# The second batch's order of attention steps: pair 8-9 first by seven half-size products, pair 6-7 scored in one step

## The chip, the cores and the metric

The kernel runs on one core of a Trainium2 chip. The metric is the device time of one execution in microseconds; the median of several runs of the kernel before is 1007.96 us. Traces count time from the start of the profiled span, and all positions below are given on that scale.

## The reference, cut to what matters

One layer on `x` of shape (2, 2048, 512), in float32: a layer norm, then a causal single-head attention and a mixture-of-experts network side by side, then a gated sum.

```python
xn = layernorm(x)
# attention (with a layer norm of its own ahead of q, k, v)
q, k, v = norm(xn) @ Wq, norm(xn) @ Wk, norm(xn) @ Wv
scores = where(causal, q @ k.T / sqrt(512), -inf)
s = softmax(scores) @ v @ o_proj + xn
# mixture of experts: top 2 of 8, y = w2 @ silu(w1 @ xn + b1) + b2
g = silu(moe(xn))
out = x + s * g
```

The change touches the attention of the second batch only: scores, softmax and the product with the values.

## The kernel before, in words

The first 567 us compute norms, projections and the experts. Then comes the attention, a loop over steps `s = 0..31`, one for each tile of 128 query rows; `seq[s]` says which tile it is. Steps 0 to 15 are the first batch, from its last tile to its first; steps 16 to 31 are the second batch, in the order 8, 9, 0, 1, 6, 7, 2, 3, 4, 5, 10 to 15. Tiles come in pairs, and two steps of one pair share the query tile `q`. Keys and values lie in blocks of 512 rows (`aks`, `avs`); tile t needs the first t + 1 groups of 128 keys.

There is no planner: each engine has a queue that it works through in the order in which the Python loop writes its instructions, and it stops at an instruction whose inputs are not there. What follows is the order of an ordinary step s. TensorE writes the scores of tile s into PSUM, chunk by chunk (`chunk_scores`, L1307), and VectorE masks the last chunk (L1312) and takes a maximum of each (`maximum`, L1295). VectorE writes the probabilities of step s - 1, which have come back transposed from a DMA, into the tile `pT` (`join_p`, L1517). Then come the row maximum `nm` (`end_scores`, L1395) and the divisor of the step before (L1659, L1660), and `exponentials`: ScalarE's exponential (L1485), GpSimd's split of the result into 16-bit halves (`pu`, L1495), and SyncE's DMA transposes (`puT`, L1501). TensorE multiplies with the values two steps late (`values`, L1535). Tiles with at most three groups of keys are turned on TensorE instead (`turn_p`, L1512). Beside this run, for older tiles: `attended` (ScalarE L1696, then VectorE L1699), `emit` (GpSimd L1707, L1708, then a store), and once for a pair `gather_y` (GpSimd's indirect DMAs, L1678) and `gate` (ScalarE L1688, VectorE L1689, ScalarE's Silu L1691).

Some pairs are multiplied by Strassen's scheme in Winograd's form, with seven half-size products for eight.

- Scores: pairs in `SCORED` take the first two key blocks by `fast_scores` (products L1359, sums of their results on VectorE L1365, one copy on ScalarE L1378). It needs sums of the key blocks (`block_sums`, tile `tk`, L1340: four subtractions, once for a batch) and of the queries (`query_sums`, tile `sq`, L1326 to L1329, once for a pair). `pair 13`, steps 26 and 27, is the first of the second batch.
- Values: pairs in `FAST` (those, and pair 4) wait until both tiles are there. `combine_p` forms sums of the two `pT` tiles (L1577, four instructions), `combine_v` those of the value blocks (tile `vT`, L1557). `values_first`, `values_next` (both in the step after the pair) and `values_end` (one step later) run seven chains of products (L1583), with VectorE's sums of the results (L1600) and one ScalarE copy (L1611).

PSUM is shared by two pools: `ps_a`, five banks, for scores and transposes, and `ps_b`, three banks, for values. Work that a later pair needs is placed by step number in the table `later`: `block_sums` of the second batch stands at steps 20 to 23, the last `combine_v` at 24 to 27.

Of the kernel before, what the change touches and what calls it, by code (L numbers as in the profile page):

```python
# [26 lines left out]
def gated_attention_moe(  # L27
# [32 lines left out]
    NT = B * S // P  # L60
    BT = 4
    TB = BT * P
    NB = NT // BT
    NBB = S // TB
# [947 lines left out]

    assert B == 2 and NBB == 4
    seq = [t for t in reversed(range(NBB * BT))]
    seq += [NBB * BT + t for t in (8, 9, 0, 1, 6, 7, 2, 3, 4, 5, 10, 11, 12, 13, 14, 15)]
    assert all(seq[s] // 2 == seq[s + 1] // 2 for s in range(0, NT, 2))
    fetch_k = fetch(aks, lambda: kp2, kt_d, "k2", "kT")
    fetch_v = fetch(avs, lambda: vp, v_d, "v2", "v")
# [249 lines left out]
    OUT = 4  # L1268


    SCORED = (0, 1, 2, 3, 13, 14, 15)
    FAST = SCORED + (4,)

    def place(s):
        b, t = divmod(seq[s], BT)
        return b, t, b - b % NBB
# [21 lines left out]
    def direct(s):  # L1298

        return range(2 if s // 2 in SCORED else 0, len(widths[s]))  # L1300

    def chunk_scores(s, j):
        b, t, first = place(s)
        w = widths[s][j]
        ps = ps_a.tile([P, TB], F32, name=f"ps_{s}_{j}", tag="a")
        for c in range(ND):
            nc.tensor.matmul(  # L1307
                ps[:, :w], lhsT=aqs[seq[s] // 2][:, c, ts(t % 2, P)], rhs=aks[first + j][:, c, :w],
                start=(c == 0), stop=(c == ND - 1),
            )  # L1310
        if first + j == b:
            nc.vector.tensor_tensor(ps[:, w - P : w], ps[:, w - P : w], keep, ALU.min)  # L1312
        maximum(s, ps[:, :w], j * TB)
# [79 lines left out]
    def end_scores(s):  # L1393
        mx, nm, pieces = scored[s]
        nc.vector.tensor_reduce(nm, mx[:, : len(pieces)], AX.X, ALU.max, negate=True)  # L1395
# [23 lines left out]
    for i in range(NM):  # L1419
# [21 lines left out]
        for _ in range(3):  # L1441
            if i >= paired.stop and early:
                f, b, c = early.pop(0)
# [115 lines left out]
    def combine_p(s, parts=(1, 3, 2, 4)):  # L1559

        m = min(min(place_keys(s), place_keys(s + 1)) // 2, MOST)
        a1, a2 = (
            turned[s + i][:, : 2 * m * P].rearrange("p (k h q) -> p k h q", h=2, q=P)
            for i in range(2)
        )
        a11, a12, a21, a22 = a1[:, :, 0], a1[:, :, 1], a2[:, :, 0], a2[:, :, 1]
        if 1 in parts:
            psums[s] = [
                cp.tile([P, MOST, P], F32, name=f"s{i}_{s}", tag=f"s{i}")[:, :m] for i in (1, 2, 4)
            ]  # L1570
        s1, s2, s4 = psums[s]
        for i, dst, x1, x2, op_ in (
            (1, s1, a21, a22, ALU.add), (3, a21, a11, a21, ALU.subtract),
            (2, s2, s1, a11, ALU.subtract), (4, s4, a12, s2, ALU.subtract),
        ):
            if i in parts:
                nc.vector.tensor_tensor(dst, x1, x2, op_)  # L1577
        combos[s] = m, a11, a12, a22, s1, s2, a21, s4
# [160 lines left out]
    K = NBB  # L1739
# [6 lines left out]
    later = {}  # L1746
    for steps, f, b in (
        ((10, 10, 11, 11), combine_v, K + 2), ((12, 12, 13, 13), combine_v, K + 1),
        ((20, 21, 22, 23), block_sums, K), ((24, 25, 26, 27), combine_v, K),
    ):  # L1750
        for i, step in enumerate(steps):
            later.setdefault(step, []).append((f, b, (i + 1,)))
# [6 lines left out]

    for s in range(NT + OUT + 2):  # L1760
        fast = s // 2 - 1 in FAST
        pair = (s, s + 1) if s // 2 in SCORED else (s,)
        if s < NT and (s % 2 == 0 or len(pair) == 1):
            for k in pair:
                if s:
                    begin_scores(k)
                room(k)
        n = s // 2 + 1
        if s % 2 == 0 and NQ <= n < NT // 2:
            for c in range(2):  # L1770
                fetch_q(n, c)
        if s == 0:
            fetch_parts(s, NBB * ND)
            block_sums(0)
        late = []
        for k in range(NT):
            if k not in AHEAD:
                wait = 4 - k % 2 if k // 2 in FAST else 3
                if s == k + wait:
                    late.append((attended, k))  # L1780
                if s == k + wait + 1:
                    emit(k)
        if s == NT:

            values_first(s - 2)
            for k in AHEAD:
                make_ahead(k)
        if len(pair) == 1 or s % 2:
            for f, *args in late:
                f(*args)  # L1790
        for k in range(NT):
            if s == (NT - 1 if k in AHEAD else k + 2 - k % 2 if k // 2 in FAST else k + 1):
                fetch_inputs(k)
        if s == NT - 1:
            gather_y(NT - 2)
        if s % 2 and s > 3 and s // 2 + 1 in SCORED:
            query_sums(s + 1, nc.vector)
        joins = []
        for k in () if s == 1 else (0, 1) if s == 2 else (s - 1,):
            if 0 <= k < NT - 1 and not by_te(k):  # L1800
                joins += [(join_p, k)] * len(halves[k])
        chunks = []
        if s < NT and s != 1:
            chunks = [(k, j) for k in ((1,) if s == 0 else (s,)) for j in direct(k)]
        if s == 0:

            for k, j in chunks:
                chunk_scores(k, j)
            chunks = []
        if s < NT and s % 2 == 0 and len(pair) == 2:  # L1810
            pools = [(ps_a, "a")] * 5 + [(ps_b, "b"), (ps_a, "a")]
            if s < 3:
                pools = [(ps_b, "b")] * 3 + [(ps_a, "a")]
            if s == 2:
                joins = [(combine_v, b, (1,)) for b in range(NBB - 1)] + joins
            now = 5 if s == 2 else 1
            fast_scores(s, pools, late + joins[:now])
            joins = joins[now:]
            if s == 0:
                query_sums(2, nc.gpsimd)  # L1820
        for k, j in chunks:
            chunk_scores(k, j)
            if s != 3 and joins:
                f, *args = joins.pop(0)
                f(*args)
        if s != 3:
            for f, *args in joins:
                f(*args)
        if 0 <= s - 1 < NT and by_te(s - 1):

            if not fast:
                values(s - 2)
            turn_p(s - 1)
        if s < NT and s != 1:
            end_scores(s)
        if fast and s % 2 == 0 and 2 < s < NT:
            combine_p(s - 2)
        if 0 <= s - 1 < NT:
            divisor(s - 1)
        if s < NT:  # L1840
            if s != 1:
                exponentials(s)
            if s % 2 == 0 and len(pair) == 2:
                maximum(s + 1, turned[s + 1][:, : 2 * TB], 0)
            if s == 0:
                end_scores(1)
                exponentials(1)
            fetch_parts(s, 4)
            for f, *args in later.pop(s, []):
                f(*args)  # L1850
        if s == 2:
            pass
        elif s == 3:
            combine_p(0, (1, 3, 2))
            for b in range(NBB - 1):
                combine_v(b, (2,))
            values_first(0)
            combine_p(0, (4,))
            for b in range(NBB - 1):
                combine_v(b, (4,))  # L1860
            values_next(0)
            for f, *args in joins:
                f(*args)
            values_end(0, [lambda: query_sums(s + 1, nc.vector)])
        elif s == NT:
            emit_ahead(s - 2, seven[s - 2][1], LO)
            values_next(s - 2)
        elif fast and s % 2 == 0:
            values_first(s - 2)

            if s != NT - 2:
                values_next(s - 2)
        elif fast and s == NT - 1:
            values_next(s - 3)
            values_end(
                s - 3,
                [lambda: join_p(s)] * len(halves[s])
                + [lambda: combine_p(s - 1, (1, 3)), lambda: gate(s - 1)]
                + [lambda: combine_p(s - 1, (2, 4))],
            )  # L1880
        elif fast:
            values_end(s - 3)
        elif 0 <= s - 2 < NT and not (s - 1 < NT and by_te(s - 1)):
            values(s - 2)

        for k in range(0, NT - 2, 2):
            if s == (k + 2 if k + 2 in AHEAD else k + 3):
                gate(k)
        for k in range(0, NT - 2, 2):
            if s == k + 1:  # L1890
                gather_y(k)
        if s == 1:

            for b in (2, 0, 1):
                combine_v(b, (3,), nc.gpsimd)
# [45 lines left out]
```

## Time and profile before

| | |
|---|---|
| runs, us | 1007.8, 1007.96, 1009.46 |
| profiled execution, us | 1007.83 |
| its span, us | 1006.0 |
| granted TensorE clock | 1.000 |
| busy: PE, VectorE, ScalarE, GpSimd | 99%, 71%, 40%, 48% |
| attention begins at | 568 us |
| second batch's first score product | 777.11 us |

In the groups and the timeline, PE is TensorE's matmul, PEld its weight load, DVE VectorE, ACT ScalarE, POOL GpSimd, and SPq the DMA queue of SyncE. A line of the timeline holds the start, the length, the engine, the source line, the operation, what it writes and reads, and how many were merged; in brackets stands the idle time before it and what ended it. A matmul's length includes the time it takes to drain, so lines of PE overlap by about 0.16 us when one follows the other at once; a break shows as a gap in the starts. One product in the source is two instructions on PE.

### The profile page before, as it was taken

The page shows a single profiled execution, that of the slowest core. Times are in us where ns is not written, and L with a number is a line of the kernel's source. Part 1 is how long each engine was busy: PE and PEld are TensorE (multiplying, and loading weights), DVE is VectorE, ACT ScalarE, POOL GpSimd, SP SyncE. Part 2 cuts the span into 40 slices and gives each one's busy share as a digit, 9 for nine tenths or more (in the row PEclk, how much of TensorE's full clock was granted, in tenths as well). Part 3 has the DMA queues.
Part 4 walks back from the last instruction along what each step waited for, and adds up shares of the span by engine and source line. Part 5 has one row for each costly group of instructions (what it writes and reads, how often), then busy time and mean ns, then how long its engine had stood idle before and what let it go on. Part 6 is the DMA issues. An engine that isn't in the chain of part 4 may idle for free. (4 is left out here: it accounts for less than half of the span.)

```text
span 1006.0 us, 13431 instructions
## 1 busy us (share of the span) xinstructions
PE 999.9 (99%) x3924; PEld 665.3 (66%) x3924; DVE 716.9 (71%) x1396; ACT 403.2 (40%) x804; POOL 483.3 (48%) x475
## 2 busy tenths in 40 slices
PE   9999999999999999999999999999999999999998
PEld 5888888874567767766753448677675544447577
DVE  6996746897887777677744579668576556878667
ACT  3344445322444454444445112232335535442241
POOL 4474564004644454444332165254557776764272
PEclk9999999999999999999999999999999999999999
DMA  8689996978999999999999576274677768753361
GB/s 293 193 264 293 329 286 258 349 249 240 202 227 220 211 208 221 217 200 222 216 218 242 164 193 147 78 206 104 183 199 239 225 200 240 207 141 86 92 165 42
DMA packets 296647, 207.96 MB, mean 207 GB/s; under 512 B 230776, under 2 KB 243832, under 8 KB 296576
## 3 DMA queue, kind: packets, MB, share of 16 engines
q1 hardware_dynamic: 282432, 163.56, 63.2%
q0 software_dynamic: 10400, 34.63, 12.5%
q10 hardware_dynamic: 3744, 8.91, 2.4%
q8 instruction: 34, 0.56, 0.2%
q14 instruction: 37, 0.30, 0.1%
HBM read 92.35 MB, written 60.03 MB: 151 GB/s over the span
## 5 line engine op out<-in xcount | busy, mean ns | idle before, releaser
L1195 PE MATMUL py<-arena,ht 128*128 (+3 forms) x396 | 176.7, 593 | 0.0
L1307 PE MATMUL ps<-k,q 128*128 128x512 f32 (+3 forms) x416 | 143.0, 495 | 0.3 <-PEq L1455 0.3
L1495 POOL COPY pu<-pT 128x1024 uint16<-128x1024 uint16 (+2 forms) x74 | 82.5, 1146 | 118.1 <-ACT pT L1485 59.1
L1166 POOL COPY hu<-h 128x704 uint16<-128x704 uint16 x66 | 61.9, 956 | 155.8 <-issue 121.7
L1195 PEld LDWEIGHTS py<-arena,ht 128*128 128x128 f32 (+3 forms) x396 | 71.8, 185 | 80.7 <-issue 76.9
L1307 PEld LDWEIGHTS ps<-k,q 128*128 128x128 f32 x416 | 74.7, 190 | 67.1 <-issue 56.5
L970 POOL DMA_INDIRECT xs<-zu_d,toki x66 | 77.6, 1176 | 70.2 <-DVE toki L791 55.6
L1181 ACT ACTIVATE ht<-ht,b1sel 128x128 f32<-128x128 f32 (+3 forms) x216 | 67.9, 380 | 88.1 <-DVE ht L1175 88.1
L1145 DVE TENSOR_TENSOR h<-p,h 128x176 f32<-128x176 f32 x182 | 55.5, 337 | 60.7 <-PE p L1138 57.2
L1678 POOL DMA_INDIRECT yg<-y_d,posi x64 | 67.4, 1053 | 36.9 <-DVE yg L1689 21.9
L1535 PE MATMUL po<-v,pT 128*128 128x512 f32 x152 | 67.9, 592 | 0.0
L347 POOL COPY zu<-z 128x1024 uint16<-128x1024 uint16 x32 | 39.9, 1245 | 55.7 <-DVE z L332 55.7
L1517 DVE COPY pT<-puT 128x1024 uint16<-128x1024 uint16 (+2 forms) x74 | 54.1, 759 | 8.8 <-DMA puT<-pu 8.6
L1485 ACT ACTIVATE pT<-pT,nm 128x1024 f32<-128x1024 f32 x14 | 16.1, 1148 | 110.3 <-DVE nm L1395 72.0
L1203 ACT COPY y<-py 128x512 f32<-128x512 f32 x55 | 32.2, 585 | 62.3 <-PE py L1195 48.4
L1485 ACT ACTIVATE pT<-ps,nm 128x512 f32<-128x512 f32 (+3 forms) x52 | 30.1, 581 | 62.5 <-DVE nm L1395 38.8
L1365 DVE TENSOR_TENSOR pT<-p,pT 128x512 f32<-128x512 f32 x49 | 32.9, 687 | 25.8 <-PE p L1359 22.1
L1535 PEld LDWEIGHTS po<-v,pT 128*128 128x128 f32 x152 | 28.6, 190 | 31.9 <-issue 30.1
L1707 POOL TENSOR_TENSOR o<-o,yg 128x512 f32<-128x512 f32 x30 | 42.0, 1398 | 14.3 <-DVE o L1699 14.1
L1699 DVE SCALAR_TENSOR_TENSOR o<-xo,xscale,o 128x512 f32<-128x512 f32 x30 | 25.9, 871 | 30.1 <-ACT o L1696 30.1
L1046 DVE COPY xT<-xhT 128x1024 uint16<-128x1024 uint16 x66 | 45.2, 712 | 2.3 <-DMA xhT<-xs 2.0
L1708 POOL TENSOR_TENSOR o<-o,xo 128x512 f32<-128x512 f32 x30 | 43.0, 1432 | 2.4
(342 smaller groups left out, 2142.9 us busy)
## 6 DMA issues: line engine op xcount, KB each, us to landing
y_d<-y SPq DMA_DIRECT2D x66, 256.0 KB, 4.4
zu_d<-zu SPq DMA_DIRECT2D x32, 264.0 KB, 2.8
kt_d<-kT SPq DMA_DIRECT2D x16, 512.0 KB, 5.9
q<-qt_d SPq DMA_DIRECT2D x32, 256.0 KB, 5.4
k<-kt_d SPq DMA_DIRECT2D x32, 256.0 KB, 4.7
v<-v_d SPq DMA_DIRECT2D x32, 256.0 KB, 5.6
xo<-in_x_dram SPq DMA_DIRECT2D x32, 256.0 KB, 3.8
x<-in_x_dram SPq DMA_DIRECT2D x30, 256.0 KB, 4.9
```

Of the source, the lines that this page charges most:

```text
L970: nc.gpsimd.indirect_dma_start(out=xs, out_offset=None, in_=zu_d, in_offset=bass.IndirectOffsetOnAxis(ap=toki[:, order[i] : order[i] + 1], ...
L1046: nc.vector.tensor_copy(xT.bitcast(U16).rearrange("p c (t h) -> p c t h", h=2), xhs.pop(i).rearrange("p (h c) t -> p c t h", h=2),)
L1145: nc.vector.tensor_tensor(out, x, y, ALU.add)
L1166: nc.gpsimd.tensor_copy(hu[:, :, :H], h.bitcast(U16).rearrange("p (d h) -> p h d", h=2))
L1181: nc.scalar.activation(ht[:hn, c, at], ht[:hn, c, at], AF.Silu, bias=b1sel[:hn, c, j : j + 1])
L1195: nc.tensor.matmul(py[at, :], lhsT=ht[:k, c, at], rhs=rhs[n], start=(c == 0), stop=(c == NH - 1),)
L1307: nc.tensor.matmul(ps[:, :w], lhsT=aqs[seq[s] // 2][:, c, ts(t % 2, P)], rhs=aks[first + j][:, c, :w], start=(c == 0), stop=(c == ND - 1),)
L1485: nc.scalar.activation(turned[s][:, at:end], src, AF.Exp, bias=nm, accum_out=rs[:, j : j + 1])
L1495: nc.gpsimd.tensor_copy(pu[:, : 2 * w].rearrange("p (h d) -> p h d", h=2), turned[s][:, k : k + w].bitcast(U16).rearrange("p (d h) -> p h ...
L1517: nc.vector.tensor_copy(turned[s][:, k : k + w].bitcast(U16).rearrange("p (i t h) -> p i t h", t=P, h=2), puT[:, : 2 * w // P, :].rearrang ...
L1535: nc.tensor.matmul(dst, lhsT=turned[s][:, ts(k, P)], rhs=avs[first + k // BT][:, k % BT, cols], start=(start and k == k0), stop=(k == k1 - 1),
L1678: nc.gpsimd.indirect_dma_start(out=y, out_offset=None, in_=y_d, in_offset=bass.IndirectOffsetOnAxis(ap=posi[k][:, n : n + 1], axis=0),)
```

## The change

The second batch is taken in the order 8, 9, 6, 7, 0, 1, 4, 5, 2, 3, 10 to 15. Pair 8 (steps 16 and 17, tiles 8 and 9) enters `SCORED`, and with it `FAST`: its scores and its values are formed by seven half-size products. `block_sums` and the last `combine_v` move ahead, to steps 14 to 17, and `query_sums` of the pair comes in step 15. Pair 9 (steps 18 and 19, tiles 6 and 7) is `JOINT`: both of its score tiles are computed in step 18, and what step 18 did for older tiles (`attended`, the joins of step 17 and the `combine_p` of pair 8) is written between the exponentials of the first and the scores of the second.

```diff
-    seq += [NBB * BT + t for t in (8, 9, 0, 1, 6, 7, 2, 3, 4, 5, 10, 11, 12, 13, 14, 15)]
+    seq += [NBB * BT + t for t in (8, 9, 6, 7, 0, 1, 4, 5, 2, 3, 10, 11, 12, 13, 14, 15)]
...
-    SCORED = (0, 1, 2, 3, 13, 14, 15)
+    SCORED = (0, 1, 2, 3, 8, 13, 14, 15)
     FAST = SCORED + (4,)
+    JOINT = (9,)
...
-        ((20, 21, 22, 23), block_sums, K), ((24, 25, 26, 27), combine_v, K),
+        ((14, 14, 15, 15), block_sums, K), ((16, 16, 17, 17), combine_v, K),
...
-        pair = (s, s + 1) if s // 2 in SCORED else (s,)
+        joint = s < NT and s // 2 in JOINT
+        pair = (s, s + 1) if s // 2 in SCORED or joint else (s,)
...
-            chunks = [(k, j) for k in ((1,) if s == 0 else (s,)) for j in direct(k)]
+            here = () if joint else (1,) if s == 0 else (s,)
+            chunks = [(k, j) for k in here for j in direct(k)]
...
-        if s < NT and s % 2 == 0 and len(pair) == 2:
+        if joint and s % 2 == 0:
+            for k in pair:
+                for j in direct(k):
+                    chunk_scores(k, j)
+                end_scores(k)
+                exponentials(k)
+                if k == s:
+                    for f, *args in late + joins:
+                        f(*args)
+                    joins = []
+                    if fast:
+                        combine_p(s - 2)
+        if s < NT and s % 2 == 0 and s // 2 in SCORED:
...
-        if s < NT and s != 1:
+        if s < NT and s != 1 and not joint:
             end_scores(s)
-        if fast and s % 2 == 0 and 2 < s < NT:
+        if fast and s % 2 == 0 and 2 < s < NT and not joint:
             combine_p(s - 2)
...
-            if s != 1:
+            if s != 1 and not joint:
                 exponentials(s)
-            if s % 2 == 0 and len(pair) == 2:
+            if s % 2 == 0 and s // 2 in SCORED:
                 maximum(s + 1, turned[s + 1][:, : 2 * TB], 0)
```

## The prediction

> **What bounds the kernel now.** I read the page first, then TensorE alone in the timeline, then all engines around 777 us, where the second batch's scores begin.
>
> ```profile
> PE 999.9 (99%) x3924; PEld 665.3 (66%) x3924; DVE 716.9 (71%) x1396; ACT 403.2 (40%) x804; POOL 483.3 (48%) x475
> PEclk9999999999999999999999999999999999999999
> PE 43%; DVE 1%; issue 0%
> ```
>
> TensorE is busy throughout at full clock, and the chain that ended last is TensorE's. So TensorE work that goes is time won, unless TensorE comes to wait. The timeline says how close that is.
>
> ```profile
> 749.20 1.03 PE L1535 MATMUL p<-v,pT 128*128 128x256 f32 x4
> 750.65 1.56 PE L1583 MATMUL p<-vT,pT 128*128 128x256 f32 x6 [0.43 <-DVE u L1600]
> ...
> 773.42 1.06 PE L1307 MATMUL ps<-k,q 128*128 128x128 f32 x8
> ...
> 777.11 7.92 PE L1307 MATMUL ps<-k,q 128*128 128x512 f32 x24
> 784.87 1.88 PE L1535 MATMUL po<-v,pT 128*128 128x512 f32 x4
> ```
>
> The 0.43 us at 750.65 is TensorE's only wait in the attention. From 777.11 on it has none: each line starts 0.16 us before the former ends. The other engines have spare time on average, but VectorE's is in pieces, and GpSimd takes part of it:
>
> ```profile
> 774.54 1.27 POOL L1707 TENSOR_TENSOR o<-o,yg 128x512 f32<-128x512 f32 x1
> 775.89 1.26 POOL L1708 TENSOR_TENSOR o<-o,xo 128x512 f32<-128x512 f32 x1
> 776.74 0.96 DVE L1699 SCALAR_TENSOR_TENSOR o<-xo,xscale,o 128x512 f32<-128x512 f32 x1 [1.92 <-ACT o L1696]
> ...
> 862.80 1.44 POOL L1707 TENSOR_TENSOR o<-o,yg 128x512 f32<-128x512 f32 x1
> 863.04 1.48 DVE L1328 TENSOR_TENSOR sq<-q 128x256 f32<-128x256 f32 x1
> 864.32 1.33 POOL L1708 TENSOR_TENSOR o<-o,xo 128x512 f32<-128x512 f32 x1
> 864.45 1.48 DVE L1329 TENSOR_TENSOR sq<-q,sq 128x256 f32<-128x256 f32 x1
> ```
>
> A `sq` subtraction takes 0.41 us alone (at 889.99), here 1.48: each ends 0.28 after the GpSimd instruction beside it (864.24 to 864.52; 865.65 to 865.93). GpSimd's add in turn ends 1.13 after `sq` (864.52 to 865.65). They alternate.
>
> **The change part by part.** A product of 512 columns is two instructions 0.429 us apart (eight take 3.43), so 0.858 us.
>
> *Removed from TensorE.* Scores of pair 8 over two blocks: 16 products become 14. Values: 16 of 512 columns over eight key groups become 28 of 256. Each saves 2 x 0.858; together **-3.43 us**. Everything else on TensorE is the same work in another order. The changed kernel's list of instructions has the seven products where the text says, so the change does what it says.
>
> *Added and moved, first wait: key and query sums (steps 14, 15).* VectorE gets two `tk` in step 14, four `sq` and two `tk` in step 15; before, the `tk` stood in steps 20 to 23, with nobody waiting. Now the third product (780.54 without a wait) needs the second `sq`, the fourth the third `tk`. A `tk` is 1.21 us:
>
> ```profile
> L1340 DVE TENSOR_TENSOR tk<-k,tk 128x1024 f32<-128x1024 f32 x2 | 2.4, 1206 | 0.0
> ```
>
> VectorE is free at 774.82 (end of step 14's L1660). Walk: `tk` waits for GpSimd until 775.81, ends 776.89; GpSimd's add until 778.02; second `tk` 779.10; L1699 779.80; `sq` 780.15; GpSimd's multiply (it needed that L1699) 781.28; second `sq` 781.56. Third product at 781.6, 1.1 us late. GpSimd's add 782.69; third and fourth `sq` 782.97, 783.3; step 15's small row work (1.0) 784.3; the last two `tk` run beside indirect DMAs, where the trace has a value subtraction at its bare 0.68 (769.15): 785.4 and 786.55. Fourth product at 785.5, another 2.1 us late. The seventh ends at 792.35 instead of 789.1: **+3.25**. Without any collision VectorE would have the third `tk` at 781.6, before the fourth product (782.26): 0.
>
> Here a rule speaks against the change. The Trainium skill, "SBUF — State Buffer", section "Who interferes with whom", says that a VectorE instruction with two SBUF inputs and a GpSimd one that reads SBUF exclude each other for a whole instruction. The rows agree on who waits, but not on the price: a blocked `sq` ends 0.28 after the release, not 0.41, a blocked add 1.13, not 1.26. By the rule alone the seven turns above would cost 0.9 us more; I take the rows.
>
> *Second wait: values of pair 8.* Before, step 18 took tiles 16 and 17 by plain `values`. Now `values_next` needs both rows transposed and summed. The chain: after the fourth `tk` come two L1689 (1.4), Silu (1.06) and the ScalarE copy of the first product (0.57, queued behind it), ending 789.5; five sums 3.41; L1699 0.75; sum, maximum over 1024, sum 2.35; mask, maximum, `nm` 0.8: exponentials of row 16 at **E = 796.85**. What follows from there is in the trace of the same tile:
>
> ```profile
> 788.48 0.69 ACT L1485 ACTIVATE pT<-ps,nm 128x512 f32<-128x512 f32 x1
> 789.32 2.82 POOL L1495 COPY pu<-pT 128x1024 uint16<-128x1024 uint16 x3 [1.35 <-ACT pT L1485]
> 790.38 3.90 SPq L1501 DMA_TRANSPOSE puT<-pu  x3
> 793.69 1.57 DVE L1517 COPY pT<-puT 128x1024 uint16<-128x1024 uint16 x1 [1.21 <-DMA puT<-pu]
> ```
>
> The third transpose starts some 4.55 after the exponential and lands 3.3 later (790.38 to 793.69). In VectorE's queue the row maximum of row 17 stands behind the three joins of row 16, so row 17's exponential starts at E + 8.9 to 9.4. In the new order ScalarE then has two L1688, a table load, Silu, another table load, two exponentials of tile 6, and only then L1696 of step 15; VectorE's L1699 waits for it, with the joins of row 17 queued behind:
>
> ```profile
> 869.22 1.33 ACT L1688 ACTIVATE yg<-yg,share 128x512 f32<-128x512 f32 x2
> 870.57 1.28 ACT L1691 ACT_TABLE_LOAD   x1
> 871.86 1.06 ACT L1691 ACTIVATE yg<-yg 128x1024 f32<-128x1024 f32 x1
> ```
>
> 1.6 (rest of row 17) + 1.35 + 1.3 + 1.0 + 1.3 + 1.25 + 0.75 + L1699 0.75 + joins 1.65 + first L1577 0.69 = 11.6. So the first sum stands at E + 20.5 to 21; each GpSimd instruction met in the joins and sums adds up to 1.1, and three may be met (E + 24.4). I take one: E + 22.1 = 819.0. TensorE without waits would want it at 777.11 + scores 12.0 + rest of steps 16 and 17 5.3 + both tiles of pair 9 12.9 + `values_first` 3.9 = 811.1. So TensorE is 7.9 late there, **4.65 more** than after the first wait. A smaller first wait doesn't help: E comes from VectorE.
>
> *Third wait.* The fourth value bank reuses the first, which is read last by L1600 behind three more L1577 (2.0), tile 7's maxima (1.8), its exponentials and the L1611 copy (1.8) and itself 0.4, all after the first sum: 6.0 against TensorE's 5.15: **+0.8**.
>
> *Moves at no cost.* Later `tk` and `vT` leave steps 20 to 27, where TensorE waited for nothing: no gain. The tiles in steps 20 to 25 keep 10 to 12 us of TensorE work between scores and values; tile 6 before had 12.3 with its join 1.2 us early, so 0 to 1 us may be lost at tile 4. The pair's `xo` loads and four `pu` and transposes change places in GpSimd's and SyncE's queues; no queue gets more. K and `q_8` are read by TensorE at 777.11 before as well. The `q` of pair 9 is issued in step 16, some 12 us ahead of use; loads of `q` there took 5.7 to 8.5.
>
> **Sum.** -3.43 + 3.25 + 4.65 + 0.8 = +5.3 us. The profiled execution took 1007.83 (span 1006.0 and 1.8 around it), 0.1 under the median: **1013.1 us**. Bounds of the unknown: no collision at all gives E = 793.3 and the first sum at 814.1, so 3.0 + 0.8 - 3.43 = +0.4; all collisions give a first sum at 821.3, so 10.2 + 1.5 (the third wait with one collision of its own) - 3.43 = +8.3.
>
> A second rule weighs on this. The skill's "TensorE: Matmul & The Clock Gate", section "Part 1: The HAM clock gate", says that an idle window of about 3.4 us halves the clock for about 3.4 us. PEclk is 9 in all slices, but the trace has no wait above 0.43 here. By the trace the second wait costs its 4.65, by the rule up to 1.7 to 3.4 more. I leave it out of the sum and put it in the range.
>
> **The rivals.**
>
> - *The cover holds (faster).* One mechanism: the 13.7 us of TensorE work between row 17's last scores and `values_first` (po, then pair 9) covers the chain of row 17. It decides at about 813.7: with the first sum there before, waits stay under 3.43 less the 0.8; at 811 the whole gain stays, 1004.5 us. For it: VectorE idles over a quarter of the time, and before, pair 26-27 ran without a wait. Against: there TensorE had 21.5 us from the end of 27's scores (887.9) to its `values_first` (909.40), and even my walk without collisions ends at 814.1. Chance 0.13.
> - *About even.* Few collisions, +0.4: 1006 to 1010 us. Chance 0.15.
> - *Waits as worked out*, 1010 to 1015.5 us, likeliest 1013.1. Chance 0.55.
> - *Long waits and the clock.* All collisions, plus up to 3.4 for the clock: 1016 to 1020 us. Chance 0.17.
>
> **How the numbers follow.** A measurement can tell 0.2%, about 2 us, from no change. Faster by more 0.13, within 0.15, slower 0.72. The range 1006.5 to 1017.5 leaves a tenth out on either side.
>
> **What would show it.** Right: TensorE gaps of about 1 and 2 us ahead of the third and fourth product (`tk`, `sq` named), one of 4 to 5 us ahead of the first L1583 with `s` in steps 18 and 19, behind L1577, and under 1 us ahead of the fourth bank; L1699 of step 15 just ahead of row 17's joins. Wrong: no gap at L1583, or gaps in steps 20 to 25, which I take as covered.

## The result, and the profile after

The changed kernel takes 1022.89 us (median of 4 runs, 1022.58 to 1023.2), the kernel before 1008.38 us beside it (4 runs, 1007.8 to 1009.46). The ratio is 1.0143, 95% interval 1.0125 to 1.016: 14.5 us slower, where 5 us slower (1013.1, range 1006.5 to 1017.5) was forecast. The sign was right, the size was not.

The profiled execution took 1023.07 us with a span of 1021.4. Line numbers of the changed kernel are one higher than those of the kernel before (L1699 is now L1700). From the page: engines, granted clock in 40 slices, and the chain that ended last.

```profile
PE 1002.0 (98%) x3950; PEld 672.5 (66%) x3950; DVE 736.7 (72%) x1417; ACT 403.3 (39%) x802; POOL 481.5 (47%) x475
PEclk9999999999999999999999999999999979999999
PE 30%; issue 5%; DVE 4%; POOL 4%; ACT 1%; DMA 1%; POOLq 0%; DVEq 0%; ACTq 0%
```

The 7 in the clock row is new, and the chain, TensorE's almost alone before, now also runs over VectorE and GpSimd. A row's busy time hides this: TensorE is still 98% busy. Its timeline (start, length, line, tiles, count; in brackets the wait ahead and what ended it) shows where:

```profile
783.69 1.99 PE L1360 MATMUL p<-tk,sq 128*128 128x512 f32 x4 [1.98 <-DVE sq L1328]
786.56 3.67 PE L1360 MATMUL p<-tk,sq 128*128 128x512 f32 x8 [0.88 <-DVE tk L1341]
...
823.77 3.75 PE L1584 MATMUL p<-vT,s 128*128 128x256 f32 x8 [8.03 <-DVE s L1578]
827.32 3.15 PE L1584 MATMUL p<-vT,pT 128*128 128x256 f32 x8
830.30 1.89 PE L1584 MATMUL p<-vT,s 128*128 128x256 f32 x8
...
868.33 4.53 PE L1536 MATMUL po<-v,pT 128*128 128x512 f32 x10
...
878.77 5.39 PE L1536 MATMUL po<-v,pT 128*128 128x512 f32 x12 [2.48 <-DVE pT L1518]
```

Beyond the bracket, each wait also cost the 0.16 us by which lines otherwise overlap. So the waits, counted from start to start, are 2.1 and 1.1 at the scores of pair 8, 8.2 at its values, 0.2 at tile 4 (868.33, too short for a bracket) and 2.6 at tile 5: 14.3 us. Then the eight instructions at 823.77 and the eight at 827.32: from start to start they take 3.55 and 2.98 us, against 1.72 at full speed. The stretches around it give the clock (columns: stretch, length, busy time and count of TensorE, its weight loads, VectorE, ScalarE, GpSimd, then the granted clock, DMA share and GB/s):

```profile
798.60:823.70 25.10, 17.13 (x51) 9.31 (x49) 19.66 (x28) 10.80 (x19) 19.44 (x16) 0.92 0.60 156
823.70:830.30 6.60, 6.53 (x17) 5.27 (x18) 4.89 (x11) 2.81 (x7) 1.97 (x2) 0.53 0.52 65
830.30:850.00 19.70, 19.70 (x74) 13.25 (x73) 12.59 (x24) 6.29 (x9) 14.07 (x12) 1.00 0.69 217
```

After the long wait TensorE ran at about half clock, which cost 1.83 + 1.26 = 3.1 us. Taken microsecond by microsecond, the granted clock fell inside the wait, some 4 us after its start (0.80 in 819 to 820), stayed at 0.50 and was back in 829 to 830 (0.58): 10.2 us in all, 6.1 of them with products to do, and half of 6.1 is the 3.1 lost. Sum: 14.3 + 3.1 - 3.43 = 14.0 of the 15.4 us by which the spans differ. Another 1.0 us of the 15.4 lies ahead of every changed step (the value product with a small wait stands at 751.65, at 750.65 before), and 0.4 I can't place.

What the long wait waits for is on VectorE and GpSimd (lines of all engines, in order of time):

```profile
808.89 3.03 POOL L1496 COPY pu<-pT 128x1024 uint16<-128x1024 uint16 x3 [2.16 <-ACT pT L1486]
809.93 2.54 DVE L1690 SCALAR_TENSOR_TENSOR yg<-yg,share,yg 128x512 f32<-128x512 f32 x2 [0.93 <-ACT yg L1689]
...
816.16 0.94 POOL L1679 DMA_INDIRECT yg<-y_d,posi  x1 [0.30 <-issue]
816.91 2.04 DVE L1700 SCALAR_TENSOR_TENSOR o<-xo,xscale,o 128x512 f32<-128x512 f32 x1 [2.86 <-ACT o L1697]
817.12 1.27 POOL L1708 TENSOR_TENSOR o<-o,yg 128x512 f32<-128x512 f32 x1
818.47 1.60 POOL L1709 TENSOR_TENSOR o<-o,xo 128x512 f32<-128x512 f32 x1
818.88 4.15 DVE L1518 COPY pT<-puT 128x1024 uint16<-128x1024 uint16 x3
820.02 2.72 POOL L1496 COPY pu<-pT 128x1024 uint16<-128x1024 uint16 x2
822.95 0.68 DVE L1578 TENSOR_TENSOR s<-pT 128x512 f32<-128x512 f32 x1
```

Read it from below. The first sum of rows, L1578, stands behind three joins, these behind L1700, and L1700 behind ScalarE, as forecast. But the VectorE instructions on the way up to the sum lie beside GpSimd ones and take longer than alone: the two L1690 beside three copies of exponentials (L1496), L1700 beside the multiply L1708, the joins beside the add L1709 and two more copies. L1690 and L1700 each end about 0.6 us after the GpSimd instruction beside them.

### The profile page after: what moved, and what is told of

Its sections match the earlier page's. It is cut to its first block, busy times and chain, and to the rows that moved or that the text cites. A ratio compares the mean times of both kernels' runs of the same rounds, so it can differ in the third digit from the quotient of the medians.

```text
span 1021.4 us, 13507 instructions
## 1 busy us (share of the span) xinstructions
PE 1002.0 (98%) x3950; PEld 672.5 (66%) x3950; DVE 736.7 (72%) x1417; ACT 403.3 (39%) x802; POOL 481.5 (47%) x475
## 5 line engine op out<-in xcount | busy, mean ns | idle before, releaser
L1496 POOL COPY pu<-pT 128x1024 uint16<-128x1024 uint16 (+3 forms) x74 | 81.5, 1134 | 123.3 <-ACT pT L1486 63.6
L1308 PE MATMUL ps<-k,q 128*128 128x512 f32 (+3 forms) x384 | 129.1, 487 | 0.3 <-PEq L1456 0.3
L1308 PEld LDWEIGHTS ps<-k,q 128*128 128x128 f32 x384 | 68.7, 190 | 59.8 <-issue 48.3
L1518 DVE COPY pT<-puT 128x1024 uint16<-128x1024 uint16 (+3 forms) x74 | 59.5, 836 | 10.1 <-DMA puT<-pu 9.0
L1366 DVE TENSOR_TENSOR pT<-p,pT 128x512 f32<-128x512 f32 x56 | 37.5, 686 | 28.1 <-PE p L1360 18.6
L1536 PE MATMUL po<-v,pT 128*128 128x512 f32 x114 | 51.4, 594 | 2.5 <-DVE pT L1518 2.5
L1486 ACT ACTIVATE pT<-ps,nm 128x512 f32<-128x512 f32 (+3 forms) x48 | 27.3, 571 | 61.5 <-DVE ri L1660 34.2
L1584 PE MATMUL p<-vT,s 128*128 128x256 f32 x180 | 43.7, 391 | 8.0 <-DVE s L1578 8.0
L1708 POOL TENSOR_TENSOR o<-o,yg 128x512 f32<-128x512 f32 x30 | 42.4, 1413 | 15.3 <-DVE o L1700 15.1
L1700 DVE SCALAR_TENSOR_TENSOR o<-xo,xscale,o 128x512 f32<-128x512 f32 x30 | 29.4, 990 | 23.6 <-ACT o L1697 21.7
L1360 PE MATMUL p<-tk,sq 128*128 128x512 f32 x96 | 42.8, 594 | 2.9 <-DVE sq L1328 2.0
```

The source lines that it names most:

```text
L1308: nc.tensor.matmul(ps[:, :w], lhsT=aqs[seq[s] // 2][:, c, ts(t % 2, P)], rhs=aks[first + j][:, c, :w], start=(c == 0), stop=(c == ND - 1),)
L1360: nc.tensor.matmul(ps, lhsT=x[:, c], rhs=y[:, c], start=(c == 0), stop=(c == ND // 2 - 1))
L1496: nc.gpsimd.tensor_copy(pu[:, : 2 * w].rearrange("p (h d) -> p h d", h=2), turned[s][:, k : k + w].bitcast(U16).rearrange("p (d h) -> p h ...
L1518: nc.vector.tensor_copy(turned[s][:, k : k + w].bitcast(U16).rearrange("p (i t h) -> p i t h", t=P, h=2), puT[:, : 2 * w // P, :].rearrang ...
L1536: nc.tensor.matmul(dst, lhsT=turned[s][:, ts(k, P)], rhs=avs[first + k // BT][:, k % BT, cols], start=(start and k == k0), stop=(k == k1 - 1),
L1584: nc.tensor.matmul(dst, lhsT=a[:, k], rhs=v(k), start=(k == 0), stop=(stop and k == n - 1))
```

## Experiments

Each is an edit of the changed kernel; ratios are to the kernel before, run beside it.

### The order alone, and the values alone

Which part of the loss belongs to the seven products, which to the order? First the new order and the joint step with pair 8 scored and valued plainly:

```diff
-    SCORED = (0, 1, 2, 3, 8, 13, 14, 15)
+    SCORED = (0, 1, 2, 3, 13, 14, 15)
-        ((14, 14, 15, 15), block_sums, K), ((16, 16, 17, 17), combine_v, K),
+        ((20, 21, 22, 23), block_sums, K), ((24, 25, 26, 27), combine_v, K),
```

> The new order and the joint step for tiles 6 and 7 alone: pair 8-9 by plain products, key sums back at steps 20 to 23, value sums at 24 to 27. Theory Q (the waits come from VectorE's queue: key and query sums in steps 14 and 15, joins and sums of pair 8 in step 18): no TensorE wait in steps 14 to 19, full clock; only tile 5's late joins (2.65 us in the changed kernel at 878.77) may remain. 1008 to 1011 us. Rival R (the new order or the joint step itself costs): over 1015 us, with waits in steps 18 and 19.

Measured: 1010.98 us, ratio 1.0035 (1.0014 to 1.0056). TensorE doesn't wait in steps 14 to 19, and the clock stays at 1.00. The order has a price of its own, about 3 us, at tiles 4 and 5:

```profile
857.24 3.24 PE L1536 MATMUL po<-v,pT 128*128 128x512 f32 x7 [1.04 <-DVE pT L1518]
...
865.96 5.39 PE L1536 MATMUL po<-v,pT 128*128 128x512 f32 x12 [0.75 <-DVE pT L1518]
```

The first line stops at the edge of its view; tile 4 has ten such instructions. Two more waits of 0.4 follow at 906 and 917. Next, scores of pair 8 by seven but values plain:

```diff
-    FAST = SCORED + (4,)
+    FAST = tuple(p for p in SCORED if p != 8) + (4,)
```

> As changed, but the values of pair 8 by plain products (scores still by seven). Theory Q: the first wait (3.3 us) stays. The wait of 8.2 us for the sums of the two probability tiles goes, since tile 8's values need row 16 alone; tile 9's values then start about 819.4 and row 17's joins ended at 823.0 in the changed kernel, so 0 to 3.6 us are waited there. Plain values cost 1.7 us. With the clock's 3.1 us gone: 1022.9 - 8.2 - 3.1 + 1.7 + 0 to 3.6 = 1013.3 to 1016.9 us. Rival (the time is lost in the scores, not in the values): 1020 us or more.

Measured: 1014.58 us, ratio 1.0068 (1.0045 to 1.0091). The long wait is gone; the first wait and tile 5's 2.6 stay. Here the first wait was followed by slow products:

```profile
783.33 2.59 PE L1360 MATMUL p<-tk,sq 128*128 128x512 f32 x4 [1.99 <-DVE sq L1328]
786.20 4.56 PE L1360 MATMUL p<-tk,sq 128*128 128x512 f32 x8 [0.28 <-DVE tk L1341]
```

In the changed kernel the same four and eight took 1.99 and 3.67 after an equal wait. The granted clock in 783 to 791 was 0.79 here (first row), 1.00 there (second row; columns as above):

```profile
783.00:791.00 8.00, 7.39 (x13) 2.84 (x14) 6.27 (x14) 5.17 (x8) 2.95 (x4) 0.79 0.85 285
783.00:791.00 8.00, 6.43 (x15) 2.76 (x16) 6.27 (x14) 5.06 (x8) 3.15 (x3) 1.00 0.80 273
```

So the clock fell around a wait of 2 us in one execution and not in the other. With plain values the loss is 6.8 us (before: 1007.75 beside it), in all 14.5, so about half of it comes with the seven products' values. The runs of this version lie 5 us apart, so the share is not known better than that.

### The clock by itself

If 3.1 us is the clock and not the wait, dummy products that fill the wait must give it back though nothing arrives sooner.

```diff
         p57 = bank(s, "p57")
+        if s == NT // 2:
+            for k in range(16):
+                nc.tensor.matmul(
+                    p57[:, LO], lhsT=combos[s][1][:, k % 4], rhs=raw(s, 0, LO)(k % 4),
+                    start=True, stop=True,
+                )
```

> As changed, but TensorE works in the long wait: 16 products of 256 columns (6.9 us) whose results the next chain overwrites stand ahead of pair 8's third chain. Theory C (the wait of 8.2 us lowers the clock, and the eight products after it pay 3.1 us): the clock stays at 1.00, the wait shrinks to about 1.3 us, nothing else moves: 1022.9 - 3.1 = 1019.8 us. Rival (the slow products after the wait have another cause, their inputs or a port): 1022.9 us, the same slow products.

Measured: 1021.68 us, but between 1018.26 and 1023.52; ratio 1.0127 (1.0108 to 1.0145). In the profiled run (1023.52, the slowest of the four) the products after the wait are at full speed:

```profile
824.02 1.99 PE L1584 MATMUL p<-vT,s 128*128 128x256 f32 x8 [0.21 <-DVE s L1578]
...
830.05 1.13 PE L1536 MATMUL p<-v,pT 128*128 128x256 f32 x4 [0.58 <-DVE o L1601]
```

From `p57` to the scores of step 20 the run needs 12.1 us, the changed kernel 13.9: 3.1 won on the clock, part of it given back by a wait for L1601, and a small one after it, that the slow products had covered. But in this run the clock fell elsewhere, to 0.79 in 783 to 791 and 0.83 in 876 to 886, at the other two waits. So all waits were filled next: 4 and 2 dummies ahead of the third and fourth product of pair 8, the 16 as above, 4 at tile 5.

```diff
+            for _ in range({3: 4, 4: 2}.get(count[0], 0) if s == NT // 2 else 0):
+                nc.tensor.matmul(ps[:, LO], lhsT=a11[:, 0], rhs=b11[:, 0, LO], start=True, stop=True)
...
+        for _ in range(4 if s == 23 else 0):
+            nc.tensor.matmul(
+                po[:, LO], lhsT=aqs[seq[25] // 2][:, 0, :P], rhs=aks[NBB][:, 0, LO],
+                start=True, stop=True,
+            )
```

> The changed kernel with dummy products in the waits: 4 and 2 of 256 columns ahead of the third and fourth score product of pair 8, 16 ahead of the seven products' values, 4 ahead of tile 5's values; their results are overwritten. If what remains of the scatter and of the loss is the clock that falls after each wait: the granted clock is 1.00 in every slice, the waits as seen on TensorE are filled, and every run lies at 1018 to 1019.5, with less than 1 us between them. Rival (the clock is not what scatters): 1021 to 1023, or runs 3 us or more apart, as with the dummy products in the long wait alone.

Measured: 1019.52 us (1018.91 to 1020.56), ratio 1.0097 (1.0067 to 1.0127), mean clock 1.00. The runs lie 1.65 us apart; less than 1 was expected. The clock's share of the loss is 1022.89 - 1019.52 = 3.4 us (3.7 if each is taken against its own runs of before), against 3.1 in the trace.

### VectorE's queue and GpSimd's turns

Two causes were left for the long wait. By theory P it is made of VectorE's collisions with GpSimd (the two engines hold each other up when they work at the same time); by theory S of latency and queue order. First, the multiply by the gate and the sum with x left out in steps 12 to 15 (the output of those tiles lacks both):

```diff
+        if not 12 <= s < 16:
             nc.gpsimd.tensor_tensor(o, o, g, ALU.mult)
             nc.gpsimd.tensor_tensor(o, o, xt, ALU.add)
```

> As changed, but GpSimd's multiply and add (the gate and the sum with x) are left out for the tiles of steps 12 to 15, so their output lacks them. Theory P (GpSimd and VectorE exclude each other, and that is most of both waits): the first wait goes (third key sum at about 782.6, needed at 783.3), row 16's exponentials start near 794.3 and not 798.6, the long wait falls from 8.2 to about 3 and keeps the clock: 1022.9 - 3.3 - 5.2 - 3.1 = 1011.3 us. Rival S (the order of VectorE's and ScalarE's queues alone makes the waits): 1019 us or more, with a long wait of 6 us or more.

Measured: 1016.65 us, ratio 1.0087 (1.007 to 1.0104), between the two theories. The long wait falls by 3.0, to 5.1 (the profiled run, 1019.24, is the slowest of four):

```profile
819.87 3.65 PE L1584 MATMUL p<-vT,s 128*128 128x256 f32 x8 [4.98 <-DVE s L1578]
```

The first wait stayed at 2.1: its collisions are with tiles of steps 10 and 11, outside the range that I had chosen. Then the queue: joins and sums of rows ahead of the attended values' scaling.

```diff
-                    for f, *args in late + joins:
+                    for f, *args in joins:
                         f(*args)
                     joins = []
                     if fast:
                         combine_p(s - 2)
+                    for f, *args in late:
+                        f(*args)
```

> As changed, but in step 18 the joins of row 17 and the sums of pair 8 stand ahead of attended of step 15, not behind it. Theory Q1 (the joins had landed and stood in VectorE's queue behind the multiply-add of attended, which waited for ScalarE's gate, two table loads and two exponentials): joins begin near 814 and not 818.9, first sum near 817 to 818, the wait of 8.2 us falls to 2 to 3.5, its clock penalty mostly goes: 1013 to 1017 us. Rival (the transposes land late, or GpSimd holds VectorE wherever the joins stand): a wait of 6 us or more, 1020 us or more.

Measured: 1020.31 us (1016.96 to 1021.01), ratio 1.0115 (1.0098 to 1.0132); less gain than expected. The trace is of the fastest run, 1016.96. The joins now start at 812.43 instead of 818.88 (all of this run lies 1.4 us earlier), but the wait only falls to 4.5:

```profile
812.43 1.31 DVE L1518 COPY pT<-puT 128x1024 uint16<-128x1024 uint16 x2
...
815.19 2.19 DVE L1518 COPY pT<-puT 128x512 uint16<-128x512 uint16 x1 [1.46 <-DMA puT<-pu]
815.82 1.27 POOL L1708 TENSOR_TENSOR o<-o,yg 128x512 f32<-128x512 f32 x1
817.17 1.33 POOL L1709 TENSOR_TENSOR o<-o,xo 128x512 f32<-128x512 f32 x1
817.31 1.75 DVE L1578 TENSOR_TENSOR s<-pT 128x512 f32<-128x512 f32 x1
```

A join of 512 columns takes 0.43 alone (at 811.14 in the last run of this series), a sum 0.68: the collisions had moved to them. And VectorE now stands idle for 1.46 us until the third transpose has landed, a part of the wait that is latency, as theory S has it. So both at once, and over all steps concerned. First the multiply and add left out in steps 10 to 23 instead of 12 to 15 (the output of those tiles lacks both, here and in the two runs that follow):

```diff
+        if not 10 <= s < 24:
             nc.gpsimd.tensor_tensor(o, o, g, ALU.mult)
             nc.gpsimd.tensor_tensor(o, o, xt, ALU.add)
```

> The changed kernel with GpSimd's multiply by the gate and sum with x (L1708, L1709 of the changed kernel) left out for the tiles of steps 10 to 23; the output of those tiles lacks the gate and the sum with x. Theory P (the collisions with GpSimd on VectorE are most of what the forecast missed): the two waits at the scores of pair 8 shrink to 0 to 0.5 us, the exponentials of row 16 start about 4 us earlier on the kernel's scale, the wait ahead of L1584 falls from 8.0 to 3 to 4 us (the place of the joins behind L1700 remains), tile 5's wait from 2.5 to 1 or less, and the clock keeps 0.9 or more in those slices: 1010 to 1013 us. Rival S (it is latency and the order of VectorE's queue, collisions are beside the point): the wait ahead of L1584 stays at 5 us or more and the time is 1017 or more.

Measured: 1013.99 us, ratio 1.0047 (1.0037 to 1.0056). The first wait is gone, tile 5's is 0.8 instead of 2.6, but the long one is 5.1, not 3 to 4. GpSimd had nothing else to do, so its copies moved up beside L1700:

```profile
812.54 2.54 DVE L1700 SCALAR_TENSOR_TENSOR o<-xo,xscale,o 128x512 f32<-128x512 f32 x1 [2.86 <-issue]
...
812.72 1.81 POOL L1496 COPY pu<-pT 128x1024 uint16<-128x1024 uint16 x2
```

Then the same with the joins ahead:

> As the run without GpSimd's two instructions in steps 10 to 23 (same part of the output left out), and with the joins of pair 8 and its sums of rows put ahead of the attended values' scaling in step 18. If queue place and collisions are the two causes and there is no third: the wait ahead of L1584 is 1.5 us or less and the time is 1006 to 1010. If a third remains (landing of the transposes, or the latency of the exponentials): the wait is 3 us or more, and the time not over 1 us below the run without the move.

Measured: 1011.16 us, ratio 1.0026 (1.0016 to 1.0035). Neither forecast was met: 2.8 us were won, but a wait of 3.2 remained. Most of it has the same cause in a new place:

```profile
811.48 2.78 DVE L1578 TENSOR_TENSOR s<-pT 128x512 f32<-128x512 f32 x1
...
811.90 1.80 POOL L1496 COPY pu<-pT 128x1024 uint16<-128x1024 uint16 x2
...
814.40 3.45 PE L1584 MATMUL p<-vT,s 128*128 128x256 f32 x8 [3.08 <-DVE s L1578]
```

So the two copies of step 18 went to ScalarE:

```diff
-                nc.gpsimd.tensor_copy(
+                (nc.scalar.copy if s == 18 else nc.gpsimd.tensor_copy)(
```

> The run with both changes (L1708 and L1709 left out in steps 10 to 23, so that those tiles lack the gate and the sum with x; joins and sums of rows ahead of the attended values' scaling), and with the two copies of the exponentials of step 18 (L1496) moved from GpSimd to ScalarE. In the run with both changes the first sum of rows (L1578) took 2.78 us in place of 0.68, beside these two copies, 811.90 to 813.70. If VectorE's collisions with GpSimd's copies are the third cause: the first sum takes 0.7 us, the wait ahead of L1584 is 1.0 us or less, the clock stays at 1.00 there, and the time is 1007 to 1009 (2.1 less for the sum, up to 1.6 less for the clock). Rival (the last transpose's landing and latency hold the sums): the wait stays at 2.5 us or more and the time at 1010.5 to 1012.

Measured: 1008.05 us, ratio 0.9997 (0.9988 to 1.0006): no difference left to the kernel before. The sum takes its bare 0.68, the wait is 1.2 (VectorE idles 1.35 for the third transpose), the clock 1.00 throughout:

```profile
811.48 0.68 DVE L1578 TENSOR_TENSOR s<-pT 128x512 f32<-128x512 f32 x1
...
812.31 1.97 PE L1584 MATMUL p<-vT,s 128*128 128x256 f32 x8 [1.03 <-DVE s L1578]
...
818.86 1.13 PE L1536 MATMUL p<-v,pT 128*128 128x256 f32 x4 [1.13 <-DVE o L1601]
...
822.34 1.99 PE L1584 MATMUL p<-vT,pT 128*128 128x256 f32 x8 [0.20 <-DVE u L1601]
```

The waits that remain (1.2 + 1.3 + 0.4) take back 2.9 of the 3.43 us. The loss is thus resolved in steps, each against its own runs of before: +14.5 as changed, +5.3 without multiply and add, +2.5 with the joins ahead as well, +0.1 with the copies on ScalarE. Part of each step is the clock: in the profiled runs products ran at 0.50 for 6.1, 5.7, 3.0 and 0 us after the long wait, and half of each is lost. The kernel before has no TensorE wait over 0.43 in this stretch, so leaving its multiply and add out could not have sped it up by more; that was not run.

### Other orders

To see whether the joint step and the order help or hurt with pair 8 by seven, the old order without the joint step:

```diff
-    (8, 9, 6, 7, 0, 1, 4, 5, 2, 3, ...)
+    (8, 9, 0, 1, 6, 7, 2, 3, 4, 5, ...)
-    JOINT = (9,)
+    JOINT = ()
```

> Pair 8 by seven products with its sums in steps 14 to 17, as changed, but in the old order (0-1 after 8-9) and with no joint step. Theory K (what covers row 17's chain is the 12.9 us of scores of tiles 6 and 7): step 18 now has 0.9 us of scores ahead of pair 8's values, so TensorE waits about as much longer as the cover is shorter, 12 us more or somewhat less since joins then wait for fewer exponentials: 1028 to 1035 us. Rival (the joint step is itself what delays the joins): no more than 1023 us.

Measured: 1028.1 us, ratio 1.0193 (1.0176 to 1.021). A wait of 5.4 comes before `values_first`, the products after it run at half clock, and the long wait stays:

```profile
819.59 3.75 PE L1584 MATMUL p<-vT,s 128*128 128x256 f32 x8 [7.81 <-DVE s L1578]
```

The new order with its joint step does serve as cover: with it the loss is 14.5 instead of some 19 us. Then, on top of the joins ahead, the key sums two steps earlier (and the K load a step earlier, the first sums of values two steps later):

```diff
-               (12, fetch_k, K), (14, fetch_v, K), ...
+               (11, fetch_k, K), (14, fetch_v, K), ...
-        ((12, 12, 13, 13), combine_v, K + 1),
-        ((14, 14, 15, 15), block_sums, K), ((16, 16, 17, 17), combine_v, K),
+        ((14, 14, 15, 15), combine_v, K + 1),
+        ((12, 12, 13, 13), block_sums, K), ((16, 16, 17, 17), combine_v, K),
```

> As the run with joins first, and the key sums in steps 12 and 13 (the key block's load moves from step 12 to 11 for it, the value sums of the block above from steps 12 and 13 to 14 and 15). Theory Q: TensorE's first wait (3.3 us) goes, as only the query sums are left ahead of the third product; row 16's exponentials come 2 to 3 us earlier, and the wait ahead of pair 8's third chain stays at 1 to 4 us. 2 to 4 us below the run with joins first: about 1011 us. Rival (key sums that wait for their load hold VectorE in steps 12 and 13, and TensorE waits there): no gain, waits near 770 to 777.

Measured: 1019.24 us, ratio 1.0096 (1.0073 to 1.0119), a miss: not told from the 1020.31 without it, as the runs of each lie 4 us apart. The third product still waits 2.0, since the query sums (L1328) stay where they were; the long wait is 5.1, and a new one of 0.7 stands at 777.69. At last the same with tiles 2, 3 ahead of 4, 5:

```diff
-    (8, 9, 6, 7, 0, 1, 4, 5, 2, 3, ...)
+    (8, 9, 6, 7, 0, 1, 2, 3, 4, 5, ...)
```

> As the run with early sums, but tiles 2 and 3 ahead of 4 and 5 again, as before the change. Theory T (the 2.65 us at tile 5's values, and 0.24 at tile 4's, come from tiles 4 and 5 having too little TensorE work behind them): those waits go and with them some clock penalties: 2.5 to 4 us below the run with early sums, about 1008 us. Rival (they come from GpSimd's and VectorE's load in those steps, whatever the tiles): no gain.

Measured: 1024.69 us, ratio 1.0151 (1.0134 to 1.0168), a miss again. Tile 3's values wait 4.8 us, because its transpose lands at 877.4 after VectorE has idled 7.4 us for it. The transpose was issued at 865.7, so 11.7 us lie in the transfer itself; why it took so long stays open.

No version that computes everything beat the kernel before, and the last version without multiply and add leaves work out and still only equals it.

## Why the prediction was wrong in size

- *Bound and gain, right.* In the trace the first two key blocks of pair 8 take 28 instructions of 512 columns for the scores, 32 before, and 56 of 256 for the values where 32 of 512 stood: eight of 512 less, 8 x 0.429 = 3.43 us.
- *First wait (+3.25), right:* 2.1 + 1.1. The walk through each turn of VectorE and GpSimd held in total, though 2.1 came at the third product and 1.1 at the fourth rather than the other way round. One multiply (778.98) went ahead of L1700 and not behind it, so the second `sq` came 1.1 later than in the walk; the number of turns up to the third key sum was the same, so the total was not touched:

```profile
776.88 2.14 POOL L1709 TENSOR_TENSOR o<-o,xo 128x512 f32<-128x512 f32 x1
777.93 2.18 DVE L1341 TENSOR_TENSOR tk<-k,tk 128x1024 f32<-128x1024 f32 x1
778.98 2.25 POOL L1708 TENSOR_TENSOR o<-o,yg 128x512 f32<-128x512 f32 x1
780.03 1.75 DVE L1700 SCALAR_TENSOR_TENSOR o<-xo,xscale,o 128x512 f32<-128x512 f32 x1
781.31 1.59 POOL L1709 TENSOR_TENSOR o<-o,xo 128x512 f32<-128x512 f32 x1
781.70 1.48 DVE L1327 TENSOR_TENSOR sq<-q 128x256 f32<-128x256 f32 x1
```

- *Second wait (+4.65), place and chain right, size wrong:* 8.2. The exponentials of row 16 start at 798.60, 0.75 later than forecast (796.85 plus the 1.0 by which this run is shifted). That is one turn at L1700 which the walk has bare:

```profile
793.58 1.27 POOL L1709 TENSOR_TENSOR o<-o,xo 128x512 f32<-128x512 f32 x1
793.79 1.60 DVE L1700 SCALAR_TENSOR_TENSOR o<-xo,xscale,o 128x512 f32<-128x512 f32 x1
```

  Row 17's exponentials follow 9.0 later, as forecast. The step that failed is "I take one": one collision of 1.1 on the rest of the chain. The walk that had been done turn by turn for the first wait was not done here. By the rows above the turns cost 1.2 at L1690 (2.54 for two instead of 1.4), of which ScalarE's Silu waited 0.7, 1.3 at L1700 and 2.5 at the joins: 4.4 on the chain. From the exponentials to the end of the first sum it took 25.0 us (20.6 bare and 4.4 in turns), 2.9 over the 22.1 taken and 0.6 over the bound of 24.4: GpSimd's copies at L1690, the multiply at L1700, and the add and two more copies at the joins fell on this chain, where I allowed for three in joins and sums and none at L1690 and L1700.
- *The bound without collisions (+0.4), not tested as it stands.* The last version of the series gives +0.1, but with other terms: its joins stand ahead, its second wait is 1.2 and not 3.0, its third 1.7 and not 0.8, and its L1690 still meet copies. That the sums agree is in part luck.
- *Third wait (+0.8), right where it can be seen.* In the changed kernel it is 0, covered by the slow products. With the clock kept up it is 0.7 and 0.2 (dummies in the long wait); with the collisions gone 1.3 and 0.4.
- *Clock (0 in the sum, up to 3.4 in the range), wrong to leave out of the sum:* 3.1 in the trace, 3.4 by the dummies. The rule of the Trainium skill ("TensorE: Matmul & The Clock Gate", "Part 1: The HAM clock gate") foresaw it, and I set it aside because the trace of before had no wait long enough to show it. That a trace doesn't contain a condition is no evidence on what the condition does. The trace differs from what I took from the rule in two points: after the long wait half clock held for 6.1 us of products, not 3.4, and the clock also fell around waits of 2.1 to 2.6 us in some runs.
- *Moves at no cost (0 to 1 us at tile 4), wrong:* 0.2 + 2.6 at tiles 4 and 5. The order alone costs about 3 us. Tile 5's wait too is mostly collisions: 0.8 without multiply and add, when its two joins take 1.04 us in place of 3.58. I named gaps in steps 20 to 25 as what would prove me wrong, and there they are.
- *The sum.* Forecast +5.3; measured +14.5. The differences: 3.5 at the second wait, 3.1 clock, 2.9 at tiles 4 and 5, less 0.8 for the hidden third wait: 8.7 of 9.2. So three steps failed: the collisions on the second chain were counted too low, the clock was put at nothing in the sum, and the waits at tiles 4 and 5 were taken as covered.

## What to carry to other kernels

Where two engines take turns, walk every instruction on the chain of a new wait, including copies that merely stand near; a count of "one" is where the largest error sat here. Removing one such neighbour let the next move into its place three times, so an experiment on it must take all of them. A TensorE wait can be paid twice, once as a wait and once in the clock: here 8.2 us of wait cost 3.1 more. So a saving of 3.43 us in products is soon lost to new waits.

## What the runs showed that I had not expected

- *A turn lost while an indirect DMA is issued.* L1700 at 816.91 started while GpSimd issued a gather (816.16 to 817.10), with no multiply running yet; the multiply started at 817.12 and ended at 818.39, and L1700 ended only at 818.95. The instruction that came first ended last. The same is seen at a join of tile 5 in the changed kernel:

```profile
876.44 3.58 DVE L1518 COPY pT<-puT 128x1024 uint16<-128x1024 uint16 x2 [0.23 <-issue]
876.79 1.27 POOL L1708 TENSOR_TENSOR o<-o,yg 128x512 f32<-128x512 f32 x1
```

  Of the other runs, those with the joins ahead (815.19, above), with plain values and without multiply and add show the same, some with GpSimd's copies in the place of the multiply. But a gather alone doesn't hold VectorE: in the last run of the series the join at 811.14 took its bare 0.43 in the middle of one (810.90 to 811.84). What decides the turn was not tested.
- *The clock after short waits.* After the first wait of 2.1 us the clock stayed at 1.00 in the profiled run of the changed kernel, and fell to 0.79 to 0.83 (in 783 to 791) in those of five other versions with the same wait. With the dummies in the long wait it was low from 785.2 to 788.6 and from 877.3 to 880.7, 3.4 us each time, against 10.2 after the long wait. What decides whether it falls was not found. It does not explain the scatter between executions: with plain values all four have a mean clock of 0.998, and they lie between 1012.41 and 1017.43 us. The kernel before, too, has single executions at 1012 and 1013 us. The cause of that scatter stays open.
- *The copies of exponentials* (uint16, one input) hold VectorE back as the multiply and add do: the sum beside them took 2.78 us, 0.68 with them on ScalarE.
